# Where GpSimd's running sums stand among VectorE's operations, in a two-layer graph kernel

## The chip, the cores and the metric

The kernel runs on one core of one Trainium2 chip. A core has five engines with a queue each: TensorE (PE in the profile; its weight loads are PEld), VectorE (DVE), ScalarE (ACT), GpSimd (POOL) and SyncE (SP, which here only starts DMA transfers). Each engine works its own queue in order; between engines there are semaphores. The metric is the device time of one execution in microseconds, the median of several runs.

## The reference

For 32 batch items of 512 nodes with 512 features, two layers are computed in float32, with one adjacency matrix `adj` for all:

```python
# layer 0: attention over the graph, 8 heads of 64
q, k, v = x @ Wq + bq, x @ Wk + bk, x @ Wv + bv
scores = einsum('bihd,bjhd->bhij', q, k) / 8 + where(adj == 0, -1e9, 0)
x = layernorm(x + einsum('bhij,bjhd->bihd', softmax(scores), v))
# layer 1: graph convolution
norm_adj = adj * deg_inv_sqrt[:, None] * deg_inv_sqrt[None, :]
x = layernorm(x + norm_adj @ (x @ weight) + bias)
```

`deg` is the row sum of `adj`. The biases are part of the computation, though they are zero in the inputs.

## The kernel before

**The attention steps.** An item's eight heads are taken two at a time, four groups per item, in the order 0, 2, 1, 3. Over 32 items that makes S = 128 steps `k`, and a last round that finishes. A step treats one group in two halves (`jj`) of two key tiles each. `scores` lets TensorE multiply keys by queries into PSUM (`sc`), VectorE clips and subtracts the mask (`e<-sc,maskT`, the operation on 128x1024), and ScalarE takes the exponential in place. `values` lets TensorE multiply the exponentials of the step before by the values (`av`); when the group is done, VectorE transposes the result (`yb<-av`) and SP sends it by four DMA transfers into the item's attention output `yT`. `accumulate` lets GpSimd add the exponentials of the four key tiles up (`acc`): one addition of two tiles for the first half, two additions onto the sum for the second, all on 128x1024 in SBUF. `sums` lets TensorE turn these sums into softmax denominators, every second step. The exponentials have six buffers (`e`), the scores two (`sc`), other products three (`mm`), the attention result one (`av`).

**The pieces beside them.** Everything else is cut into pieces, Python tuples of a cost, a function and its arguments. A piece with a cost of 2.1 is one of the seven products by which `seven` makes a 512x512 matrix product out of 256x256 quarters, or one of four parts of the product with the adjacency. `values_of` and `keys_and_queries` make the next item's values, keys and queries. `turn` and `combine` transpose the item after it (`xT`) and form differences of its quarters on GpSimd. `finish(b)` gives layer 0's end for item b: `inverse` (reciprocals `inv` of the denominators), `add` (VectorE multiplies `yT` by `inv`, GpSimd adds the residual `xr`), `measure` (statistics, `st` and `mv`), `root` (`ve` and `nmu` on VectorE, `rstd` and `add` on GpSimd), `judge` (three small checks on the reciprocals), `norm` (ScalarE: `yT` normalised, then `hi`, a rounded copy scaled by the degrees), `split` (VectorE: `lo`, what `hi` left out; then GpSimd adds the bias `b1` to `yT`), `grow` (ScalarE). `convolve(b)` gives layer 1: `first` (four parts, `hi` and `lo` times `adjT`, copied by ScalarE to `zT`), `parts` (differences of `zT`'s quarters, GpSimd), `second` (seven products with the weight, added into `y` by VectorE and GpSimd), `measure`, `root` and `store`.

**What sets the order.** The order of every engine's queue is the program's. Once per item, at `at == 1`, the list `side` of pieces is written out by hand: the dictionary `beside` says after which product the pieces without cost stand. At the end of each of the four following steps, `run(side, share)` takes pieces from the list until a quarter of the remaining cost is done. It stops right after the product that reaches its due, so pieces without cost that stand behind it begin the next stretch. `accumulate` is called around `scores`: the first half's addition right before the scores of the second half, the second half's two additions right after these, in any case before the stretch.

**The end.** Item 31 has no next item. Its sums go to separate tiles, in the space of weights that are done with. Its softmax is finished in two halves, `early` for two groups and `late` for the other two (`add_half`), and its product with the adjacency goes row tile by row tile (`block`, `unload`). `held` is item 29's second layer, whose products are kept for steps 125 to 127. After the last round, lines of `run` write out the order of the rest. If the last check of a count (`bad`) is over zero, a general second kernel follows; with these inputs it does not run.

Of the kernel before, what the change touches and what calls it, by code (L numbers as in the profile page):

```python
# [9 lines left out]
F32 = mybir.dt.float32  # L10
# [3 lines left out]
AF = mybir.ActivationFunctionType  # L14
ALU = mybir.AluOpType
AX = mybir.AxisListType

P = 128
# [31 lines left out]
def unshifted(  # L50
# [29 lines left out]
    B, N, D = x.shape  # L80
    NT = N // P
    DT = D // P
    G = H // 2
    SCALE = 1.0 / HD**0.5
    tensor, vector, scalar, gpsimd = (InOrder(tc, e) for e in (nc.tensor, nc.vector, nc.scalar, nc.gpsimd))

    consts = ctx.enter_context(tc.tile_pool(name="consts", bufs=1))
    acts = ctx.enter_context(tc.tile_pool(name="acts", bufs=2))
# [14 lines left out]
    XT = consts.tile([P, 7, 2, HALF], F32, name="xT")  # L103
# [27 lines left out]
    R = {}  # L131

    def load_residual(b):

        if b < B - 2:
            t = acts.tile([P, NT, D], F32, name="xr", tag="zT", bufs=1)
            R[b] = [t[:, i, :] for i in range(NT)]
        else:
            t = XT if b == B - 2 else wk
            R[b] = [t[:, i].rearrange("p u o -> p (u o)") for i in range(NT)]  # L140
        for i in range(NT):
            nc.sync.dma_start(R[b][i], x[b, ts(i, P), :])

# [36 lines left out]
    wk = load_parts(Wk, "wk", nc.sync)  # L180
# [57 lines left out]
    bias = consts.tile([P, 2, DT], F32, name="bias")  # L238
# [111 lines left out]
            )  # L350
            scalar.activation(e, e, AF.Exp)

    def accumulate(s):


        b, g, jj = s
        n = 2 * ORDER.index(g) + jj
        a = None
        if b == B - 1:
            if n > 1:  # L360
                t, at = ((wq, 0), (wq, 2), (wq, 4), (wk, 4), (wv, 4), (XT, 4))[n - 2]
                a = t[:, at : at + 2].rearrange("p k u o -> p k (u o)")
        if a is None and (jj == 0 or b == B - 1):
            a = work.tile([P, 2, N], F32, name="acc", bufs=2)
        if a is not None:
            ACC.setdefault((b, g), []).append(a)
            gpsimd.tensor_add(a, E[s][0], E[s][1])
        else:
            for l in range(2):
                gpsimd.tensor_add(ACC[b, g][0], ACC[b, g][0], E[s][l])  # L370

    def values(s):
# [74 lines left out]
    def finish(b):  # L447


        t = {}  # L450
# [48 lines left out]
        def norm(i):  # L499
            if i == 0:  # L500
                if b < B - 1:
                    HI[b], LO[b] = (acts.tile([P, NT, D], F32R, name=k, bufs=1) for k in ("hi", "lo"))
                    LO[b] = [LO[b][:, k, :] for k in range(NT)]
                else:
                    HI[b] = acts.tile([P, NT, D], F32R, name="hi2", tag="v")
                    lo = [acts.tile([P, 2, D], F32R, name="lo2", tag="kq", bufs=5) for _ in range(2)]
                    LO[b] = [lo[k // 2][:, k % 2, :] for k in range(NT)]
            x1 = YT[b][:, i, :]
            scalar.activation(
                x1, x1, AF.Identity, bias=t["add"][:, i : i + 1], scale=t["rstd"][:, i : i + 1]  # L510
            )

            scalar.activation(HI[b][:, i, :], x1, AF.Copy, scale=dis[:, i : i + 1])

# [11 lines left out]
        def block(f):  # L526
# [3 lines left out]
            early=[(0.6, inverse, ((0,),))] + [(0, add_half, (i, 0)) for i in range(NT)],  # L530
            late=[(0.6, inverse, ((1,),))] + [(0, add_half, (i, 1)) for i in range(NT)],
            inverse=[(0.6, inverse, ((0, 1),))], add=block(add), measure=block(measure), root=[(0, root, ())],
            judge=[(0, judge, ())], norm=block(norm), split=block(split), grow=block(grow),
        )

    def weave(side, main):

        out, done = [], 0
        for k, piece in enumerate(main):
            due = len(side) * (k + 1) // len(main)  # L540
            out += side[done:due] + [piece]
            done = due
        return out + side[done:]
# [106 lines left out]
            stores=[(0, store, (n, n - n % 2)) for n in range(NT)],  # L650
        )

    def run(pieces, share=1.0):

        due = share * sum(c for c, _, _ in pieces)
        done = 0
        while pieces and (done < due or share == 1.0):
            c, f, args = pieces.pop(0)
            f(*args)
            done += c  # L660

    ORDER = (0, 2, 1, 3)
    blocks = [(b, g) for b in range(B) for g in ORDER]
# [17 lines left out]
    run(weave(masks, keys_and_queries(0, 1)))  # L681
    one, two = turns(1)
    run(one)
    side, rest, held = [], [], None
    for k in range(S + 1):
        b, at = divmod(k, G)
        if at == 1:
            run(side)
            if b:
                load_residual(b - 1)  # L690
            if b + 2 < B:
                load_x(b + 2, 0)
            if b + 1 < B:
                main, kq = values_of(b + 1) + keys_and_queries(b + 1, 0), keys_and_queries(b + 1, 1)
                turn0, turn1 = turns(b + 2) if b + 2 < B else ([], [])
                main += kq[:5]
            if b == 0:
                w1_parts = [(0, weigh_part, (w1, gpsimd, i)) for i in range(4)]
                side = main[:7] + [(0, degrees, ())] + weave(w1_parts, main[7:]) + turn0 + kq[5:] + turn1
            elif b < B - 1:  # L700
                f, c = finish(b - 1), convolve(b - 1)
                norm, split, grow = f["norm"], f["split"], f["grow"]
                add, measure = f["add"], f["measure"]

                beside = {
                    0: rest[:1], 1: rest[1:2], 2: rest[2:3], 4: rest[3:4], 5: rest[4:5] + f["inverse"],
                    6: rest[5:6] + add[:2], 7: rest[6:] + add[2:], 9: measure[:2], 10: measure[2:3],
                    11: measure[3:] + f["root"], 12: f["judge"], 13: norm[:2], 14: norm[2:3] + split[:1],
                    15: norm[3:] + split[1:2], 16: split[2:3], 17: split[3:], 18: turn0,
                }  # L710
                side = sum(([piece] + beside.get(i, []) for i, piece in enumerate(main)), [])
                side += c["first"] + c["parts"] + grow + kq[5:] + turn1[:1]
                if b < B - 2:
                    s = c["second"]
                    side += s[:1] + turn1[1:2] + s[1:4] + turn1[2:3] + s[4:5] + turn1[3:4]
                    side += s[5:6] + c["measure"][:1] + turn1[4:] + s[6:] + c["measure"][1:2]
                    rest = c["measure"][2:] + c["root"] + c["store"]
                else:
                    held = c
            else:  # L720
                f, c = finish(b - 1), convolve(b - 1)
                s, norm, split, add = held["second"], f["norm"], f["split"], f["add"]

                ending = {
                    S - 3: s[:1] + f["inverse"] + s[1:2] + add[:2] + s[2:3] + add[2:],
                    S - 2: s[3:4] + f["measure"][:2] + s[6:] + f["measure"][2:] + f["root"] + f["judge"],
                    S - 1: s[4:5] + norm[:3] + split[:1] + s[5:6] + norm[3:] + split[1:],
                    S: [],
                }


        if k == S - 2:
            load_residual(B - 1)
        if k < S:
            scores((*blocks[k], 0))
        if k:
            values((*blocks[k - 1], 0))
            values((*blocks[k - 1], 1))
            if k % 2 == 0:
                sums(blocks[k - 1][0], (k - 1) % G // 2)  # L740
        if k < S:
            accumulate((*blocks[k], 0))
            scores((*blocks[k], 1))
            accumulate((*blocks[k], 1))
        if k == 0:
            run(two)
        if k >= S - 3:
            run(ending[k])
        else:
            run(side, 1.0 / (G - (at - 1) % G))  # L750
        if k == S - 1:
            last = finish(B - 1)
            run(last["early"])

    end, e = last, convolve(B - 1)
    s, first, norm, split, block, add = c["second"], c["first"], end["norm"], end["split"], e["block"], end["late"][1:]
    run(first[:1] + end["late"][:1] + add[:2] + first[1:2] + add[2:] + first[2:3] + end["measure"][:2] + first[3:])
    run(end["measure"][2:] + end["root"] + c["parts"] + f["grow"] + held["measure"] + s[:1] + norm[:1] + s[1:2])
    run(norm[1:2] + split[:1] + s[2:3] + block[:1] + norm[2:3] + split[1:2] + s[3:4] + block[1:2] + norm[3:])
    run(split[2:3] + s[4:5] + block[2:3] + split[3:] + block[3:] + e["unload"] + e["parts"] + s[5:] + end["grow"])  # L760
    run(held["root"] + end["judge"])

# [9 lines left out]
    vector.memset(ones, 1.0)  # L774

    s, tail = e["second"], c["measure"] + c["root"] + c["store"]
    run(held["store"] + s[:1] + tail[:1] + s[1:2] + tail[1:2] + s[2:3] + tail[2:3] + s[3:4] + tail[3:5] + s[4:5])
    p = ps_mm.tile([1, 1], F32, name="mm")
    tensor.matmul(p, count, ones, start=True, stop=True)
    vector.tensor_scalar(bad, p, -1.0, float(P * B * NT * H + N), op0=ALU.mult, op1=ALU.add)  # L780
# [285 lines left out]
```

## Time and profile before

| | |
|---|---|
| Three runs | 2954.48, 2954.88, 2959.91 us (median 2954.88) |
| Profiled execution | 2955.07 us; span 2953.2 us |
| TensorE busy | 2872.4 us, 97% of the span |
| VectorE / GpSimd / ScalarE busy | 2057.9 / 1819.9 / 1062.3 us |
| One item in the middle (1074.03 to 1164.38) | 90.35 us |
| VectorE `lo`, mean of 124 | 1.464 us |
| VectorE `yT<-yT,inv`, mean of 124 | 1.249 us |
| GpSimd `acc<-acc,e`, mean of 248 | 2.534 us |
| GpSimd `acc<-e`, mean of 126 | 2.354 us |

In the profile, an operation is named by what it writes and reads (`lo<-yT,dis,hi`). All operations go through one recording helper, so they have its line, L44, and are told apart by these names. The bracket at the end of a line of the timeline gives the idle time of that engine before the line, and what ended it. A line with "x4" covers four operations with their pauses. Matmuls overlap, so their lengths add up to more than their time; the distance from start to start counts. `w` is the weight of layer 1, `b_r` its bias (`bv_r` the bias of the values). For item 31, `yT` lies in `wv`, its residual in `wk` and its `zT` and `parts` in `xT`, and the names in the trace are these.

### The profile page before, as it was taken

The numbers are of one execution on the slowest core, as the hardware profiler recorded it, in microseconds if no ns is written. First come the engines' busy times: TensorE is split into PE (matmuls) and PEld (weight loads), VectorE is DVE, ScalarE is ACT, GpSimd is POOL, SyncE is SP. The second block draws the span as 40 slices with busy tenths as digits, with TensorE's granted clock in tenths as the row PEclk, the third lists the DMA queues.
The fourth block names the chain that finished last, engine by engine and source line by source line (L and its number), as shares of the span: only waits on it lengthen the run. The fifth ranks groups of instructions, "written<-read, shape, count | busy, mean of one in ns | idle before, by whom it ended". The sixth has DMA issues, their size and how long they took to land.

```text
span 2953.2 us, 35448 instructions
## 1 busy us (share of the span) xinstructions
PE 2872.4 (97%) x12966; PEld 1878.3 (64%) x12966; DVE 2057.9 (70%) x2908; ACT 1062.3 (36%) x1342; POOL 1819.9 (62%) x1141
## 2 busy tenths in 40 slices
PE   7999999999999999999999999999999999999997
PEld 5666666666666666666666666666666666666655
DVE  7667766677667677666776676776767766677766
ACT  1233333343333333333433333333334334333243
POOL 3666566656666665666566666656665666666565
PEclk9999999999999999999999999999999999999998
DMA  5111222111222111221112221112211222211121
GB/s 130 31 26 47 49 56 50 43 36 47 54 51 47 40 47 47 57 50 43 35 49 54 50 47 40 47 47 57 48 40 39 50 54 51 46 41 47 40 47 48
DMA packets 383398, 142.40 MB, mean 48 GB/s; under 512 B 280048, under 2 KB 349680, under 8 KB 383216
## 3 DMA queue, kind: packets, MB, share of 16 engines
q1 hardware_dynamic: 381920, 138.75, 19.8%
q8 instruction: 104, 1.70, 0.2%
q10 hardware_dynamic: 1296, 1.31, 0.2%
q14 instruction: 78, 0.64, 0.1%
HBM read 72.88 MB, written 33.55 MB: 36 GB/s over the span
## 4 chain that ended last, share of the span: by engine, by line
PE 80%; DVE 15%; issue 4%; DMA 1%; ACT 0%; POOL 0%; SPq 0%; DVEq 0%; POOLq 0%; ACTq 0%
PE mm L44 50%; PE av L44 15%; PE sc L44 15%; DVE e L44 5%; DVE yT L44 3%; DVE lo L44 3%; DVE u L44 1%; DVE kq L44 1%; DMA x<-in_x_dram 0%; DVE xT L44 0%; DVE wv L44 0%; DVE st L44 0%; DVE y L44 0%; ACT yT L44 0%; ACT hi L44 0%
## 5 line engine op out<-in xcount | busy, mean ns | idle before, releaser
L44 ACT ACTIVATE e<-e 128x1024 f32<-128x1024 f32 x512 | 541.2, 1057 | 896.7 <-DVE e L44 806.4
L44 POOL TENSOR_TENSOR acc<-acc,e 128x1024 f32<-128x1024 f32 x248 | 628.5, 2534 | 126.0 <-ACT e L44 116.1
L44 DVE SCALAR_TENSOR_TENSOR e<-sc,maskT 128x1024 f32<-128x1024 f32 x512 | 601.7, 1217 | 117.3 <-PE sc L44 117.2
L44 POOL TENSOR_TENSOR acc<-e 128x1024 f32<-128x1024 f32 x126 | 296.6, 2354 | 517.3 <-ACT e L44 273.8
L44 PE MATMUL sc<-kq 64*128 64x512 f32 x2048 | 509.8, 615 | 6.4 <-DVE e L44 6.4
L44 PE MATMUL mm<-xT,wk 128*128 128x256 f32 x1792 | 474.7, 387 | 12.4 <-DVE kq L44 10.4
L44 PE MATMUL av<-e,v 128*64 128x512 f32 x2048 | 467.7, 598 | 0.0
L44 PE MATMUL mm<-xT,wq 128*128 128x256 f32 x1792 | 460.8, 380 | 0.0
L44 PE MATMUL mm<-wv,xT 128*128 128x256 f32 x1792 | 403.0, 382 | 15.2 <-DVE xT L44 11.5
L44 PEld LDWEIGHTS mm<-xT,wk 128*128 128x128 f32 x1792 | 328.0, 190 | 138.9 <-issue 74.0
L44 PEld LDWEIGHTS mm<-wv,xT 128*128 128x128 f32 x1792 | 336.3, 191 | 84.1 <-issue 26.6
L44 PEld LDWEIGHTS mm<-xT,wq 128*128 128x128 f32 x1792 | 341.1, 190 | 46.6
L44 PEld LDWEIGHTS sc<-kq 64*128 64x128 f32 x2048 | 175.9, 186 | 277.0 <-issue 187.0
L44 PEld LDWEIGHTS av<-e,v 128*64 128x64 f32 x2048 | 135.5, 136 | 315.8 <-issue 298.2
L44 POOL TENSOR_TENSOR yT<-yT,xr 128x512 f32<-128x512 f32 x120 | 161.7, 1368 | 179.2 <-DVE yT L44 173.0
L44 PE MATMUL mm<-w,zT 128*128 128x256 f32 x992 | 224.8, 379 | 0.0
L44 PE MATMUL mm<-adjT,lo 128*128 128x512 f32 x496 | 200.0, 403 | 25.2 <-DVE lo L44 25.2
L44 POOL TENSOR_TENSOR yT<-yT,b_r 128x512 f32<-128x512 f32 x124 | 170.9, 1399 | 75.4 <-DVE lo L44 75.4
L44 DVE STREAM_TRANSPOSE yb<-av 128x512 f32<-128x512 f32 x128 | 91.7, 716 | 176.7 <-PE av L44 176.7
L44 DVE SCALAR_TENSOR_TENSOR lo<-yT,dis,hi 128x512 fp32r<-128x512 f32 x124 | 181.5, 1464 | 39.8 <-ACT hi L44 39.8
L44 PEld LDWEIGHTS mm<-w,zT 128*128 128x128 f32 x992 | 188.2, 190 | 27.1 <-issue 1.5
L44 DVE TENSOR_TENSOR kq<-u,mm 128x512 f32<-128x512 f32 x128 | 86.4, 675 | 170.4 <-PE mm L44 170.3
(123 smaller groups left out, 3170.3 us busy)
## 6 DMA issues: line engine op xcount, KB each, us to landing
x<-in_x_dram SPq DMA_DIRECT2D x256, 128.0 KB, 2.9
out_dram<-y SPq DMA_DIRECT2D x128, 256.0 KB, 2.1
yT<-yb SPq DMA_DIRECT2D x496, 64.0 KB, 2.5
xr<-in_x_dram SPq DMA_DIRECT2D x120, 256.0 KB, 3.5
wv<-in_L_gnn_Wv_dram ACTq DMA_DIRECT2D x8, 128.0 KB, 4.7
wk<-in_L_gnn_Wk_dram SPq DMA_DIRECT2D x8, 128.0 KB, 4.1
wq<-in_L_gnn_Wq_dram SPq DMA_DIRECT2D x8, 128.0 KB, 4.5
yT<-in_adj_dram SPq DMA_DIRECT2D x1, 1024.0 KB, 6.6
```

Of the source, the lines that this page charges most:

```text
L44: return self.tc.keep_in_program_order(op(*args, **kwargs))
```

## The change

- **The second half's sums are put off.** For all items but the last, `accumulate` of the second half is no longer called at once. Its two additions go to a list, `pending`, one entry each, and a piece `more` issues one of them where `put_off` stands in the order. What is left is issued at the top of the next step.
- **Stretches end with all their pieces.** `run` takes whole lists. `cut` deals `side` into four lists by the number of products (pieces with a cost over 1), and the pieces behind a stretch's last product belong to that stretch.
- **The order in an item is written anew.** All of `add` comes in the first stretch, all of `norm`, `split` and `judge` in the second. The two additions put off stand: in the first stretch behind the third and the fifth product, in the second behind `measure` and `root`, in the third behind its first two products, in the fourth around the first product of `second`. `grow` goes ahead of the first layer-1 product. The statistics and stores of the item two back come together in the first stretch.
- **The end is dealt out anew.** Item 30's residual has tiles of its own (in the space of `x` and of one `kq`), and is loaded after step 123. Its `inverse` and `add` go to step 124 with the first three products of `held`; the other four, `measure`, `root`, `norm` and half of `split` to step 125; the rest of `split`, the early half of item 31, item 30's `first` and `parts` to step 126; `held`'s statistics and stores and two products of item 30's `second` to step 127. Every second `norm` of item 31 scales on VectorE instead of ScalarE.

```diff
-        else:
-            t = XT if b == B - 2 else wk
-            R[b] = [t[:, i].rearrange("p u o -> p (u o)") for i in range(NT)]
+        elif b == B - 2:
+            t = [acts.tile([P, 2, D], F32, name="xr2", tag=tag, bufs=n) for tag, n in (("x", 1), ("kq", 5))]
+            R[b] = [t[i // 2][:, i % 2, :] for i in range(NT)]
+        else:
+            R[b] = [wk[:, i].rearrange("p u o -> p (u o)") for i in range(NT)]
...
-    def accumulate(s):
+    def accumulate(s, ls=(0, 1)):
...
-            for l in range(2):
+            for l in ls:
                 gpsimd.tensor_add(ACC[b, g][0], ACC[b, g][0], E[s][l])
...
+            if b == B - 1 and i % 2:
+                vector.tensor_scalar(x1, x1, rstd, add, op0=ALU.mult, op1=ALU.add)
+            else:
+                scalar.activation(x1, x1, AF.Identity, bias=add, scale=rstd)
...
-    def run(pieces, share=1.0):
-        due = share * sum(c for c, _, _ in pieces)
-        done = 0
-        while pieces and (done < due or share == 1.0):
-            c, f, args = pieces.pop(0)
+    def run(pieces):
+        for _, f, args in pieces:
             f(*args)
-            done += c
+    def cut(pieces, counts):
+        lists = [[]]
+        left = list(counts)
+        for piece in pieces:
+            if piece[0] > 1:
+                if not left[0]:
+                    left.pop(0)
+                    lists.append([])
+                left[0] -= 1
+            lists[-1].append(piece)
+        return lists
+    pending = []
+    def more():
+        if pending:
+            accumulate(*pending.pop(0))
...
                 beside = {
-                    0: rest[:1], 1: rest[1:2], 2: rest[2:3], 4: rest[3:4], 5: rest[4:5] + f["inverse"],
-                    6: rest[5:6] + add[:2], 7: rest[6:] + add[2:], 9: measure[:2], 10: measure[2:3],
-                    11: measure[3:] + f["root"], 12: f["judge"], 13: norm[:2], 14: norm[2:3] + split[:1],
-                    15: norm[3:] + split[1:2], 16: split[2:3], 17: split[3:], 18: turn0,
+                    0: rest[:1], 1: rest[1:3], 2: put_off, 3: rest[3:4], 4: rest[4:5] + put_off,
+                    5: rest[5:6] + f["inverse"], 6: rest[6:] + add[:2], 7: add[2:],
+                    8: measure[:2] + put_off, 9: measure[2:], 10: f["root"] + put_off, 11: norm[:1],
+                    12: norm[1:2] + split[:1], 13: norm[2:3] + split[1:2], 14: norm[3:] + split[2:3],
+                    15: split[3:] + f["judge"], 16: put_off + grow[:2], 17: put_off + grow[2:], 18: turn0,
                 }
...
+                    side += put_off + s[:1] + put_off + s[1:3] + turn1[1:2] + s[3:4] + turn1[2:3] + s[4:5]
+                    side += turn1[3:4] + s[5:6] + c["measure"][:1] + turn1[4:] + s[6:] + c["measure"][1:2]
+                    shares = cut(side, (8, 8, 8, 8))
                 else:
-                    held = c
+                    held, h, last = c, s, finish(b)
+                    add = last["add"]
+                    side += h[:1] + last["inverse"] + h[1:2] + add[:2] + h[2:3] + add[2:]
+                    shares = cut(side, (8, 8, 8, 4))
...
-                ending = {
-                    S - 3: s[:1] + f["inverse"] + s[1:2] + add[:2] + s[2:3] + add[2:],
-                    S - 2: s[3:4] + f["measure"][:2] + s[6:] + f["measure"][2:] + f["root"] + f["judge"],
-                    S - 1: s[4:5] + norm[:3] + split[:1] + s[5:6] + norm[3:] + split[1:],
-                    S: [],
-                }
+                shares = [
+                    h[3:4] + f["measure"][:2] + h[6:] + f["measure"][2:] + f["root"] + h[4:5] + f["judge"] + norm[:2]
+                    + h[5:6] + split[:1] + norm[2:] + split[1:2],
+                    split[2:] + last["early"][:1] + first[:1] + add[:2] + first[1:2] + add[2:] + first[2:]
+                    + c["parts"] + f["grow"],
+                    held["measure"] + held["root"] + s[:2] + held["store"],
+                    [],
+                ]
+        while pending:
+            more()
...
-            accumulate((*blocks[k], 1))
+            if b == B - 1:
+                accumulate((*blocks[k], 1))
+            else:
+                pending += [((*blocks[k], 1), (l,)) for l in range(2)]
+        if k == S - G - 1:
+            load_residual(B - 2)
...
-        if k >= S - 3:
-            run(ending[k])
-        else:
-            run(side, 1.0 / (G - (at - 1) % G))
-        if k == S - 1:
-            last = finish(B - 1)
-            run(last["early"])
+        elif shares:
+            run(shares.pop(0))
...
-    run(first[:1] + end["late"][:1] + add[:2] + first[1:2] + add[2:] + first[2:3] + end["measure"][:2] + first[3:])
-    run(end["measure"][2:] + end["root"] + c["parts"] + f["grow"] + held["measure"] + s[:1] + norm[:1] + s[1:2])
-    run(norm[1:2] + split[:1] + s[2:3] + block[:1] + norm[2:3] + split[1:2] + s[3:4] + block[1:2] + norm[3:])
-    run(split[2:3] + s[4:5] + block[2:3] + split[3:] + block[3:] + e["unload"] + e["parts"] + s[5:] + end["grow"])
-    run(held["root"] + end["judge"])
+    run(s[2:3] + end["late"][:1] + add[:2] + s[3:4] + add[2:] + s[4:5] + end["measure"] + end["root"] + s[5:6])
+    run(norm[:2] + split[:1] + block[:1] + norm[2:3] + split[1:2] + block[1:2] + norm[3:] + split[2:3] + block[2:3])
+    run(split[3:] + block[3:] + e["unload"] + e["parts"] + s[6:] + end["grow"] + end["judge"])
...
-    run(held["store"] + s[:1] + tail[:1] + s[1:2] + tail[1:2] + s[2:3] + tail[2:3] + s[3:4] + tail[3:5] + s[4:5])
+    run(s[:1] + tail[:1] + s[1:2] + tail[1:2] + s[2:3] + tail[2:3] + s[3:4] + tail[3:5] + s[4:5])
```

More of the change, by code (lines that the diff above doesn't have):

```diff
@@ L508, in norm @@
             x1 = YT[b][:, i, :]
-            scalar.activation(
-                x1, x1, AF.Identity, bias=t["add"][:, i : i + 1], scale=t["rstd"][:, i : i + 1]
-            )
+            rstd, add = t["rstd"][:, i : i + 1], t["add"][:, i : i + 1]
+            if b == B - 1 and i % 2:
+                vector.tensor_scalar(x1, x1, rstd, add, op0=ALU.mult, op1=ALU.add)
+            else:
+                scalar.activation(x1, x1, AF.Identity, bias=add, scale=rstd)
             scalar.activation(HI[b][:, i, :], x1, AF.Copy, scale=dis[:, i : i + 1])
@@ L683, in unshifted @@
     run(one)
-    side, rest, held = [], [], None
+    shares, rest = [], []
     for k in range(S + 1):
@@ L687, in unshifted @@
         if at == 1:
-            run(side)
-            if b:
+            if 0 < b < B - 1:
                 load_residual(b - 1)
@@ L699, in unshifted @@
                 side = main[:7] + [(0, degrees, ())] + weave(w1_parts, main[7:]) + turn0 + kq[5:] + turn1
+                shares = cut(side, (6, 5, 5, 5))
             elif b < B - 1:
@@ L703, in unshifted @@
                 add, measure = f["add"], f["measure"]
+                put_off = [(0, more, ())]
                 beside = {
-                    0: rest[:1], 1: rest[1:2], 2: rest[2:3], 4: rest[3:4], 5: rest[4:5] + f["inverse"],
-                    6: rest[5:6] + add[:2], 7: rest[6:] + add[2:], 9: measure[:2], 10: measure[2:3],
-                    11: measure[3:] + f["root"], 12: f["judge"], 13: norm[:2], 14: norm[2:3] + split[:1],
-                    15: norm[3:] + split[1:2], 16: split[2:3], 17: split[3:], 18: turn0,
+                    0: rest[:1], 1: rest[1:3], 2: put_off, 3: rest[3:4], 4: rest[4:5] + put_off,
[3 more added lines that the diff above has]
+                    15: split[3:] + f["judge"], 16: put_off + grow[:2], 17: put_off + grow[2:], 18: turn0,
@@ L710, in unshifted @@
                 }
                 side = sum(([piece] + beside.get(i, []) for i, piece in enumerate(main)), [])
-                side += c["first"] + c["parts"] + grow + kq[5:] + turn1[:1]
+                side += c["first"] + c["parts"] + kq[5:] + turn1[:1]
+                s = c["second"]
                 if b < B - 2:
-                    s = c["second"]
-                    side += s[:1] + turn1[1:2] + s[1:4] + turn1[2:3] + s[4:5] + turn1[3:4]
-                    side += s[5:6] + c["measure"][:1] + turn1[4:] + s[6:] + c["measure"][1:2]
+                    side += put_off + s[:1] + put_off + s[1:3] + turn1[1:2] + s[3:4] + turn1[2:3] + s[4:5]
+                    side += turn1[3:4] + s[5:6] + c["measure"][:1] + turn1[4:] + s[6:] + c["measure"][1:2]
@@ L717, in unshifted @@
                     rest = c["measure"][2:] + c["root"] + c["store"]
+                    shares = cut(side, (8, 8, 8, 8))
                 else:
-                    held = c
-            else:
-                f, c = finish(b - 1), convolve(b - 1)
-                s, norm, split, add = held["second"], f["norm"], f["split"], f["add"]
-                ending = {
-                    S - 3: s[:1] + f["inverse"] + s[1:2] + add[:2] + s[2:3] + add[2:],
-                    S - 2: s[3:4] + f["measure"][:2] + s[6:] + f["measure"][2:] + f["root"] + f["judge"],
-                    S - 1: s[4:5] + norm[:3] + split[:1] + s[5:6] + norm[3:] + split[1:],
-                    S: [],
-                }
+                    held, h, last = c, s, finish(b)
@@ new lines, in unshifted @@
+                    add = last["add"]
+                    side += h[:1] + last["inverse"] + h[1:2] + add[:2] + h[2:3] + add[2:]
+                    shares = cut(side, (8, 8, 8, 4))
+            else:
+                f, c, last = last, convolve(b - 1), finish(b)
+                s, first, norm, split, add = c["second"], c["first"], f["norm"], f["split"], last["early"][1:]
+                shares = [
[6 more added lines that the diff above has]
+                ]
@@ L743, in unshifted @@
             scores((*blocks[k], 1))
-            accumulate((*blocks[k], 1))
+            if b == B - 1:
[4 more added lines that the diff above has]
+            load_residual(B - 2)
         if k == 0:
             run(two)
-        if k >= S - 3:
-            run(ending[k])
-        else:
-            run(side, 1.0 / (G - (at - 1) % G))
-        if k == S - 1:
-            last = finish(B - 1)
-            run(last["early"])
-    end, e = last, convolve(B - 1)
-    s, first, norm, split, block, add = c["second"], c["first"], end["norm"], end["split"], e["block"], end["late"][1:]
-    run(first[:1] + end["late"][:1] + add[:2] + first[1:2] + add[2:] + first[2:3] + end["measure"][:2] + first[3:])
-    run(end["measure"][2:] + end["root"] + c["parts"] + f["grow"] + held["measure"] + s[:1] + norm[:1] + s[1:2])
-    run(norm[1:2] + split[:1] + s[2:3] + block[:1] + norm[2:3] + split[1:2] + s[3:4] + block[1:2] + norm[3:])
-    run(split[2:3] + s[4:5] + block[2:3] + split[3:] + block[3:] + e["unload"] + e["parts"] + s[5:] + end["grow"])
-    run(held["root"] + end["judge"])
+        elif shares:
+            run(shares.pop(0))
+    end, e = last, convolve(B - 1)
+    norm, split, block, add = end["norm"], end["split"], e["block"], end["late"][1:]
+    run(s[2:3] + end["late"][:1] + add[:2] + s[3:4] + add[2:] + s[4:5] + end["measure"] + end["root"] + s[5:6])
+    run(norm[:2] + split[:1] + block[:1] + norm[2:3] + split[1:2] + block[1:2] + norm[3:] + split[2:3] + block[2:3])
+    run(split[3:] + block[3:] + e["unload"] + e["parts"] + s[6:] + end["grow"] + end["judge"])
     count = small.tile([P, 1], F32, name="count")
```

## The prediction

> **What bounds the kernel now.** I read the page's busy shares first, then the windows over one batch item, then the waits of TensorE, then the order of time around each wait. The page and one item's window (columns: length, busy us with counts, granted clock, DMA share, GB/s):
>
> ```profile
> PE 2872.4 (97%) x12966; PEld 1878.3 (64%) x12966; DVE 2057.9 (70%) x2908; ACT 1062.3 (36%) x1342; POOL 1819.9 (62%) x1141
> 1074.03:1164.38 90.35, 89.27 (x405) 58.44 (x405) 63.07 (x89) 33.19 (x42) 56.75 (x36) 1.00 0.20 47
> 1164.38:1254.74 90.36, 89.27 (x404) 58.44 (x405) 63.09 (x89) 33.20 (x42) 56.81 (x36) 1.00 0.20 47
> ```
>
> Items repeat to 0.01 us, and in each TensorE lacks work for 90.35 - 89.27 = 1.08 us. The waits view (total, times, longest) says for whom, once per item:
>
> ```profile
> PE mm L44 <- DVE lo L44: 25.2, 30, 1.1
> PE mm L44 <- DVE kq L44: 10.4, 30, 3.0
> PE sc L44 <- DVE e L44: 6.4, 4, 2.8
> ```
>
> The timeline shows why VectorE is late: first the `kq` wait, then the `lo` wait (start, length, engine):
>
> ```profile
> 1160.27 3.45 DVE L44 TENSOR_TENSOR yT<-yT,inv 128x512 f32<-128x512 f32 x2
> 1160.46 5.49 POOL L44 TENSOR_TENSOR acc<-acc,e 128x1024 f32<-128x1024 f32 x2 [1.14 <-ACT e L44]
> 1163.65 0.67 DVE L44 TENSOR_TENSOR kq<-e,mm 128x512 f32<-128x512 f32 x1
> ...
> 1092.03 5.57 POOL L44 TENSOR_TENSOR acc<-acc,e 128x1024 f32<-128x1024 f32 x2 [0.21 <-ACT e L44]
> 1093.10 2.26 DVE L44 SCALAR_TENSOR_TENSOR lo<-yT,dis,hi 128x512 fp32r<-128x512 f32 x1
> 1096.06 2.09 DVE L44 SCALAR_TENSOR_TENSOR lo<-yT,dis,hi 128x512 fp32r<-128x512 f32 x1
> 1098.21 0.50 PE L44 MATMUL mm<-adjT,lo 128*128 128x512 f32 x1 [0.82 <-DVE lo L44]
> ```
>
> Two products by `inv` take 3.45 us here and 1.29 at 1149.24, where GpSimd is idle; `lo` takes 2.26 beside a running sum and 0.75 alone (1083.16). VectorE instructions with one operand in PSUM keep 0.69 beside the same sums. The last `kq` ends 0.25 us and the last `lo` 0.82 us after TensorE needed it: that is the 1.08.
>
> [...] the lengths above are 0.65 to 0.75 plus a rest of a 2.35 us sum. When both queues are full they alternate: four `inv` products took 7.87 us at 2784.96 beside two sums and a residual addition. [...] here a 2.95 us wait is followed by matmuls of 1.91 and 1.72 us instead of 1.03 (2794.60)[...].
>
> **The change, part by part: items 1 to 29.** TensorE's order is the same there; what moves is the order on VectorE, ScalarE and GpSimd. A piece (one product of seven) takes 1.73 us of TensorE.
>
> *First stretch.* All four `inv` products now stand in it, after its seventh piece, beside residual additions only (1.27 us each). Taking turns: 4 x 0.65 + 2 x 1.27 = 5.1 us from 1149.24, so the mask step `e` starts near 1154.4 instead of 1151.43 and its halves end near 1155.6 and 1156.75. TensorE needs those score buffers at 1156.76 and 1157.7: about 1 us of slack, cost nothing. The layer norm's `rstd` now precedes the two sums on GpSimd, so these run near 1142.9 to 1147.7 (before: 1137.59 to 1142.4) and meet `u<-u,bv_r`, which has two SBUF inputs: it waits from 1143.7 to about 1145, and the matmul buffer that piece seven needs at 1146.71 is free at about 1146.9. Estimate 0.15 us an item (0 to 0.3).
>
> *Second stretch* (old time 1158.67 to 1172.5). Without the `inv` products VectorE takes `kq` at 1160.5: 0.25 us gained. The statistics (0.8 us a pair, one SBUF input) are unhindered by the first sum; `rstd` and its partner `add` end near 1167.4. The second sum follows them, 1167.4 to 1169.8, so the first `lo` (ready at 1169.0) waits 0.7 us. ScalarE's four norms with `hi` last to about 1174.2. The other three `lo` wait for at most one addition of `b1` (1.27) each: last end near 1175.1, the judging's three small instructions 0.5, `e` at 1175.7 to 1178.0. TensorE needs the two score buffers at 1178.0 and 1179.0; the halves are free at 1176.9 and 1178.0. Slack 1 us; cost nothing, bounds 0 and, if every `lo` loses a turn to one more addition, 1.3 - 1.0 = 0.3, or 2 us if several do.
>
> *Third stretch.* No `lo` is left, so first products find their operands: 0.82 us gained. GpSimd's sums stand there before `parts`, as before. *Fourth:* the order of one `xT` difference against one `y` addition; TensorE didn't wait there before; nothing. Four stores instead of three plus one are issued earlier on SP, before the `yb` transfers that follow 9 us later; nothing.
>
> Sum: 29 x (1.08 - 0.15) = 27.0 us. In item 0 the halves of the sum now stand behind other GpSimd work, up to 5.1 us, and TensorE asks for them a step later: nothing.
>
> **The end: items 30 and 31.** Let T be the end of the last attention matmul, 2883.64.
>
> *Up to T.* From 2783.3 to T are 100.34 us, of which 9.7 are lost: `kq` 2.95 plus 1.8 of slow matmuls, 1.02, 1.12, and 2.83 for `e` at 2873.77. With all `inv` products early and stretches of eight pieces the first three go, together 6.9. The last stays: the stretch of step 125 holds measures, root, norms and two `lo`, and GpSimd's `y` additions (2.5 us, behind a sum) still hold up VectorE. From the old lengths `e` starts 15.3 us after that stretch's start, and TensorE has 14.3 us of work: 2.3 us lost. In step 126 the two remaining `lo` come after both `e` and beside sums: some 3 us lost, and I add 0.7 for the clock. So 6.0 instead of 9.7. But four first products (7.45 us) and two second ones (3.46) now lie before T: T moves by 10.9 + 6.0 - 9.7 = +7.2.
>
> *After T.* Before:
>
> ```profile
> 2886.28 5.22 DVE L44 TENSOR_TENSOR wv<-wv,inv 128x128 f32<-128x128 f32 x8
> 2891.42 0.70 DVE L44 STREAM_TRANSPOSE yb<-av 128x512 f32<-128x512 f32 x1
> 2907.36 3.45 PE L44 MATMUL mm<-w,parts 128*128 128x256 f32 x8 [3.10 <-POOL parts L44]
> 2928.80 2.93 ACT L44 ACTIVATE y<-y,add,rstd 128x512 f32<-128x512 f32 x4 [3.82 <-POOL add L44]
> 2932.23 0.69 DVE L44 TENSOR_TENSOR y<-wv,mm 128x512 f32<-128x512 f32 x1 [3.35 <-ACT e L44]
> ```
>
> The transposition waited 7.8 us behind the early half's products, which go to step 126: it now starts near T+0.3. Its four transfers queue on SP behind four stores, which wait for ScalarE until about T+2.4; they land near T+6.9 (before: 2896.56, T+12.9). From landing to the layer norm's factors took 8.05 us; two `mm` evacuations and two `y` additions now stand in between, 3.0: T+18. Then 2.4 us (norm, `hi`, `lo`: 0.8 + 0.7 + 0.75 and handing over) to the first block instead of 5.8, since `parts` are long made: T+20.4 against T+26.8. Four blocks (7.4), one second product (1.7) and 1.8 for a slow clock after ten idle us: T+31.3 against 2925.20, T+41.6. The rest took 28.0; ScalarE's four stores of item 29 no longer stand before the copy of `e`, worth 3.5: T+56 against T+69.6. That is -13.5, with the move of T -6.3. Bounds: -14 if step 126 loses nothing, +4 if both `lo` wait for whole sums and the slow clock lasts.
>
> Total 27.0 + 6.3 = 33.3 from the profiled span of 2953.2: 2919.9; the median run, 2954.88, is 1.7 above that span, so 2921.6, rounded 2922. The other runs lie at 2954.48 and 2959.91.
>
> **The rivals.**
> - *Queueing eats half.* VectorE's fuller first and second stretches cost TensorE 0.5 us an item. For it: slacks are only 1 us. Against: the additions that collide are half as long as the sums. 29 x 0.58 + 4 = 21: 2934.
> - *The wait only changes place.* The second sum and `b1` additions hold `lo` so long that about 1 us an item remains; the change then does not do what it says. Only the end gains: 2949.
> - *Slower.* In the second stretch, `lo` loses turns to additions of `b1` so that `e` comes late. It decides from 2.3 us behind my schedule: 1 us of slack, 1.08 gained and 0.2 from the end. At three more additions, 3.8 us, the loss is 2.8 - 1.08 = 1.7 an item, +50 - 6: 2999. Against: pairs of waiting `lo` got through between two additions at 2882.32.
> - *The end fails:* items gain, but step 126 stalls cold: +8 there, 2936.
>
> **How the numbers follow.** Mine 0.58, half eaten 0.18, end fails 0.08, wait moved 0.07, slower 0.09. Nothing under 0.2% (6 us) can be told from no change. Mine runs from 2908 (no new wait, end -14) to 2930; taking in the half and the failed end gives 2908 to 2942. The moved wait sits at the edge of 0.2%, so: faster 0.88, same 0.03, slower 0.09.
>
> **What would show it.** Items of 89.3 to 89.6 us; TensorE's waits for `lo` and `kq` gone; `yT<-yT,inv` mean below 1.0 us, `lo` below 1.2 (before 1.25 and 1.46); sums near 2.4 instead of 2.53; the last `yb` within 1 us of the last `av`; no wait for `parts`. I'm wrong if TensorE waits for `e` or `mm` buffers once an item, or if the stretch from T exceeds 60 us.

## The result, and the profile after

The changed kernel takes 2935.02 us (median; 2934.62 to 2935.12) against 2954.68 for the kernel before: 19.7 us less, ratio 0.9929 with a 95% interval of 0.9912 to 0.9946. The forecast was 2922, with a range of 2908 to 2942. So the direction and the range held, but the gain is 60% of the forecast 33 us, about where the rival "queueing eats half" stood (2934). The prediction's own case ended at 2930; the range reached 2942 only because rivals were taken in.

The page's busy shares of the changed kernel, and the windows over two items:

```profile
PE 2871.6 (98%) x12966; PEld 1881.9 (64%) x12966; DVE 2080.2 (71%) x2910; ACT 1057.7 (36%) x1340; POOL 1812.6 (62%) x1141
1065.10:1154.94 89.84, 89.29 (x406) 58.63 (x404) 63.90 (x90) 32.96 (x42) 56.46 (x36) 1.00 0.20 48
1085.12:1175.00 89.88, 89.32 (x406) 58.67 (x406) 63.93 (x90) 33.01 (x43) 56.55 (x35) 1.00 0.20 47
```

TensorE's work is the same; an item is 0.5 us shorter, where 0.93 was forecast. The waits of TensorE show that the old two are gone and that others have come:

```profile
PE sc L44 <- DVE e L44: 17.0, 33, 2.8
PE sc L44 <- ACT hi L44: 11.2, 1, 11.2
PE mm L44 <- DVE e L44: 8.0, 32, 1.4
```

No wait for `lo` or `kq` is left. Two are new in every item: `sc` for `e` (17.0 us, 33 times), and `mm` for `e` (8.0 us, 32 times; this `e` is the one that empties a buffer of products). The 11.2 us is at the end, before the first block. The timeline shows what runs beside the late instructions. First the edge of the second and third stretch (1080.71 on), then the first stretch; lines of other operations are left out:

```profile
1080.71 1.60 DVE L44 SCALAR_TENSOR_TENSOR lo<-yT,dis,hi 128x512 fp32r<-128x512 f32 x1 [0.66 <-ACT hi L44]
1082.24 0.17 DVE L44 TENSOR_SCALAR low<-inv 128x32 f32<-128x32 f32 x1
1082.40 1.27 POOL L44 TENSOR_TENSOR yT<-yT,b_r 128x512 f32<-128x512 f32 x1 [0.63 <-DVE lo L44]
1082.44 1.27 DVE L44 SCALAR_TENSOR_TENSOR low<-inv,low 128x32 f32<-128x32 f32 x1
1083.85 2.35 DVE L44 SCALAR_TENSOR_TENSOR e<-sc,maskT 128x1024 f32<-128x1024 f32 x2
1085.12 2.26 PE L44 MATMUL sc<-kq 64*128 64x512 f32 x8 [0.37 <-DVE e L44]
...
1138.52 5.14 POOL L44 TENSOR_TENSOR acc<-acc,e 128x1024 f32<-128x1024 f32 x2
1139.65 1.78 DVE L44 TENSOR_TENSOR u<-u,bv_r 128x512 f32<-128x512 f32 x1
1142.97 1.97 PE L44 MATMUL mm<-wv,xT 128*128 128x256 f32 x8 [0.18 <-DVE e L44]
```

The check `low<-inv,low` handles 32 elements per partition and takes 1.27 us, as long as the addition of `b1` beside it, and the mask step `e`, which stands behind the checks in VectorE's queue, is late. In the first stretch `u<-u,bv_r` takes 1.78 us instead of 0.69, beside the first put-off sum. That the instruction beside them is what they wait for is tested below. The groups of operations, means in ns after the comma, say that this is so in nearly all items:

```profile
L44 DVE SCALAR_TENSOR_TENSOR lo<-yT,dis,hi 128x512 fp32r<-128x512 f32 x124 | 149.8, 1227 | 46.5 <-ACT hi L44 46.5
L44 DVE TENSOR_TENSOR u<-u,bv_r 128x512 f32<-128x512 f32 x32 | 55.5, 1736 | 1.1
L44 DVE SCALAR_TENSOR_TENSOR low<-inv,low 128x32 f32<-128x32 f32 x32 | 38.6, 1205 | 1.1
L44 POOL TENSOR_TENSOR acc<-acc,e 128x1024 f32<-128x1024 f32 x248 | 597.4, 2409 | 64.1 <-ACT e L44 54.2
```

In the kernel before, the second and the third line were:

```profile
L44 DVE TENSOR_TENSOR u<-u,bv_r 128x512 f32<-128x512 f32 x32 | 24.4, 764 | 1.1
L44 DVE SCALAR_TENSOR_TENSOR low<-inv,low 128x32 f32<-128x32 f32 x32 | 6.1, 192 | 1.1
```

**A better yardstick than idle time.** The ends of matmuls in a profile are modelled, so the idle gap before a matmul can understate a loss: TensorE's gap for `kq` was 0.25 us, but without that wait its interval is 0.55 shorter. Each step has one `av` group, and the distance from start to start of these groups shows the whole loss. In the timelines they start at 1084.81, 1107.88, 1130.31, 1152.18 and 1175.16 in the kernel before, and at 1103.79, 1126.22, 1148.51, 1170.94 and 1193.63 in the changed one. So an item divides as follows (us; the interval is named by the stretch that lies in it, and what the end of one stretch delays shows in the next interval):

| kernel | first | second | third | fourth | item |
|---|---|---|---|---|---|
| before | 21.87 | 22.98 | 23.07 | 22.43 | 90.35 |
| changed | 22.29 | 22.43 | 22.69 | 22.43 | 89.84 |
| changed, both new waits mended (below) | 21.87 | 22.43 | 21.99 | 22.42 | 88.71 |

So, measured against the last line, the old waits cost 0.55 + 1.08 = 1.63 us an item, not 1.08, and the new ones cost 0.42 + 0.70 = 1.12, not 0.15.

### The profile page after: what moved, and what is told of

It reads as the page before. It is cut to its first block, busy times and chain, and to the rows that moved or that the text cites. A ratio compares the mean times of both kernels' runs of the same rounds, so it can differ in the third digit from the quotient of the medians.

```text
span 2933.2 us, 35519 instructions
## 1 busy us (share of the span) xinstructions
PE 2871.6 (98%) x12966; PEld 1881.9 (64%) x12966; DVE 2080.2 (71%) x2910; ACT 1057.7 (36%) x1340; POOL 1812.6 (62%) x1141
## 4 chain that ended last, share of the span: by engine, by line
PE 73%; DVE 16%; ACT 6%; issue 2%; POOL 2%; DMA 1%; SPq 0%; DVEq 0%; POOLq 0%; ACTq 0%
PE mm L44 47%; PE sc L44 15%; PE av L44 12%; DVE u L44 3%; ACT yT L44 3%; DVE e L44 3%; DVE st L44 3%; ACT hi L44 2%; DVE lo L44 2%; DVE low L44 1%; POOL rstd L44 1%; ACT e L44 1%; DVE mv L44 1%; DVE kq L44 1%; DVE v L44 1%
## 5 line engine op out<-in xcount | busy, mean ns | idle before, releaser
L44 POOL TENSOR_TENSOR acc<-acc,e 128x1024 f32<-128x1024 f32 x248 | 597.4, 2409 | 64.1 <-ACT e L44 54.2
L44 PE MATMUL sc<-kq 64*128 64x512 f32 x2048 | 521.2, 623 | 17.1 <-DVE e L44 17.0
L44 POOL TENSOR_TENSOR yT<-yT,xr 128x512 f32<-128x512 f32 x124 | 193.6, 1591 | 80.6 <-DVE yT L44 80.6
L44 POOL TENSOR_TENSOR rstd<-ve,minus_half 128x4 f32<-128x4 f32 (+1 forms) x65 | 65.6, 1009 | 252.8 <-DVE nmu L44 252.7
L44 PE MATMUL mm<-adjT,hi 128*128 128x512 f32 x496 | 201.9, 407 | 0.0
```

The lines of the kernel that those rows point to most:

```text
L44: return self.tc.keep_in_program_order(op(*args, **kwargs))
```

## The experiments

Two theories. A: the new order itself is good, and two or three instructions of VectorE that it put beside GpSimd take back what it gains. B: the gain comes from putting the sums off, and what is missing is VectorE's fuller queue as such. Nine runs, each timed beside the kernel before. The executions of one variant lie up to 3.5 us apart (those of the kernel before up to 6), so a difference of 1 or 2 us says nothing.

**1. The checks elsewhere.** In the changed kernel, `judge` moves from the end of the second stretch to behind product 9 (counted from 0 over the item, the second of that stretch), where GpSimd is idle:

```diff
-                    8: measure[:2] + put_off, 9: measure[2:], 10: f["root"] + put_off, 11: norm[:1],
+                    8: measure[:2] + put_off, 9: measure[2:] + f["judge"], 10: f["root"] + put_off, 11: norm[:1],
...
-                    15: split[3:] + f["judge"], 16: put_off + grow[:2], 17: put_off + grow[2:], 18: turn0,
+                    15: split[3:], 16: put_off + grow[:2], 17: put_off + grow[2:], 18: turn0,
```

> The changed kernel, with the three checks of judge moved from the end of the second stretch to its ninth product, where GpSimd is idle between a sum and rstd. Theory A (two operations with two SBUF inputs that the new order put beside GpSimd cost most of what the items should have gained: the check low<-inv,low behind an addition of b1, and u<-u,bv_r behind a put-off sum): the check takes 0.19 us instead of 1.27, e comes 1.1 us sooner, TensorE's wait for e before the second scores goes; 0.6 us an item, 2917 (2913 to 2923). Theory B (VectorE's second stretch is simply too full; what is gained is gained by putting the sums off): the last lo is as late as before, the wait stays, 2932 to 2936.

Measured: 2912.48 us, ratio to the kernel before 0.9855 (0.9839 to 0.9872). That is 22.5 below the changed kernel, a little more than A expected and against B. The timeline, at the same place:

```profile
1073.22 1.60 DVE L44 SCALAR_TENSOR_TENSOR lo<-yT,dis,hi 128x512 fp32r<-128x512 f32 x1 [0.72 <-ACT hi L44]
1074.75 2.34 DVE L44 SCALAR_TENSOR_TENSOR e<-sc,maskT 128x1024 f32<-128x1024 f32 x2
1074.90 1.28 POOL L44 TENSOR_TENSOR yT<-yT,b_r 128x512 f32<-128x512 f32 x1 [0.63 <-DVE lo L44]
1076.66 1.99 PE L44 MATMUL sc<-kq 64*128 64x512 f32 x8
```

The last `lo` is as slow as before (1.60), but `e` follows it at once, runs beside the addition of `b1` at its full pace, and `sc` waits for nothing. The slack that the prediction counted on is there; the checks had used it up.

**2. The first stretch's sums ahead of `rstd`.** Both put-off sums go behind the first product:

```diff
-                    0: rest[:1], 1: rest[1:3], 2: put_off, 3: rest[3:4], 4: rest[4:5] + put_off,
+                    0: put_off + put_off + rest[:1], 1: rest[1:3], 3: rest[3:4], 4: rest[4:5],
```

> The changed kernel, with both put-off sums of the first stretch behind its first product, ahead of rstd on GpSimd, as before the change. Theory A: u<-u,bv_r takes 0.7 to 0.8 us instead of 1.74, TensorE's wait for the buffer of the seventh product goes; 0.4 us an item, 2923 (2920 to 2928). Theory B: sums back beside VectorE's work, no gain or a loss: 2935 to 2945.

Measured: 2922.50 us, ratio 0.9888 (0.9872 to 0.9905), 12.5 below the changed kernel. A holds:

```profile
L44 DVE TENSOR_TENSOR u<-u,bv_r 128x512 f32<-128x512 f32 x32 | 24.3, 761 | 1.1
```

**3. Nothing put off.** All sums are issued at once; stretches and order stay:

```diff
-            if b == B - 1:
-                accumulate((*blocks[k], 1))
-            else:
-                pending += [((*blocks[k], 1), (l,)) for l in range(2)]
+            accumulate((*blocks[k], 1))
```

> The changed kernel, with every second-half sum issued at once, as before the change; stretches and the new order stay. Theory A: the putting off gains nothing by itself, since the new order of add, norm and split already keeps the two-input operations away from the sums; u<-u,bv_r is free again, so faster than the changed kernel: 2925 (2920 to 2932). Theory B: the items lose what they had gained, 2945 to 2955.

Measured: 2913.94 us, ratio 0.9861 (0.9845 to 0.9877): 21.1 below the changed kernel, more than A expected. Putting the sums off, the first part of the change, costs 21 us in this order. 12.5 of them lie in the first stretch (experiment 2). Most of the other 8.6 lie at the edge of the second and third, whose interval is 22.44 instead of 22.69 here:

```profile
1065.01 1.02 POOL L44 TENSOR_TENSOR rstd<-ve,minus_half 128x4 f32<-128x4 f32 x1 [0.92 <-DVE nmu L44]
1067.94 0.75 DVE L44 SCALAR_TENSOR_TENSOR lo<-yT,dis,hi 128x512 fp32r<-128x512 f32 x1 [0.81 <-ACT hi L44]
```

Both sums of this step are over before `rstd` (they end at 1064.09); the first `lo` takes 0.75. In the changed kernel one sum follows `rstd`, and that `lo` takes 1.23:

```profile
1073.93 2.36 POOL L44 TENSOR_TENSOR acc<-acc,e 128x1024 f32<-128x1024 f32 x1
1075.61 1.23 DVE L44 SCALAR_TENSOR_TENSOR lo<-yT,dis,hi 128x512 fp32r<-128x512 f32 x1 [0.81 <-ACT hi L44]
```

**4. The new end alone.** Items 0 to 29 are those of the kernel before, with its `beside` and sums at once, and a stretch stops right after its last product (`cut_early` begins a new list there):

```diff
-                    shares = cut(side, (8, 8, 8, 8))
+                    shares = cut_early(side, (8, 8, 8, 8))
```

> The kernel before in items 0 to 29 (sums at once, old order, stretches that stop at their last product) with the new end from item 30 on. Theory A, by the prediction's sum for the end: 6 us faster than before, 2949 (2945 to 2952), items of 90.35 us. Rival: the end gives nothing and all 20 us come from the items: 2954 to 2956.

Measured: 2949.07 us, ratio 0.9979 (0.9971 to 0.9987), 6.0 below the kernel before (2955.06 in these runs). The items have the old intervals (22.99, 23.07). The end is worth about what the prediction's sum said, 6.3.

**5. The new end and the rule for stretches.** As 4, with `cut` as in the change (pieces behind a stretch's last product belong to it), the old places of the pieces and sums at once.

> The kernel before in its items (sums at once, old places of the pieces) with the new end, and with stretches that end with all their pieces: the run with the new end alone plus one rule. Theory A: the second two products by inv now stand in the first stretch, so TensorE's wait for kq goes (0.43 us an item by the distance of matmul starts), the wait for lo stays since two lo still stand beside the sums of the third stretch: 29 x 0.43 = 12 us below the new end alone, 2937 (2933 to 2941). Rival: the products by inv now delay e before the second scores, nothing gained: 2947 to 2951.

Measured: 2922.53 us, ratio 0.9888 (0.9872 to 0.9905): 26.5 below experiment 4, twice what was expected. The second interval falls to 22.43, as expected, by 0.55 rather than 0.43. The third falls too, to 22.71. In the kernel before, the second of the four `lo` stood at the head of the third stretch (1091.84); now it ends the second (1075.59 here), and the last two, though still beside the sums, come sooner:

```profile
1075.59 0.75 DVE L44 SCALAR_TENSOR_TENSOR lo<-yT,dis,hi 128x512 fp32r<-128x512 f32 x1
...
1083.16 5.15 POOL L44 TENSOR_TENSOR acc<-acc,e 128x1024 f32<-128x1024 f32 x2 [0.98 <-ACT e L44]
1084.01 2.06 DVE L44 SCALAR_TENSOR_TENSOR lo<-yT,dis,hi 128x512 fp32r<-128x512 f32 x1
1086.78 2.09 DVE L44 SCALAR_TENSOR_TENSOR lo<-yT,dis,hi 128x512 fp32r<-128x512 f32 x1
```

From the start of `av` (1075.88) to the end of the last `lo` are 12.99 us, against 13.34 before (1084.81 to 1098.15); the interval is 0.36 shorter.

Experiments 4, 5 and 3 and the changed kernel form a ladder: end -6.0, rule -26.5, new order of the pieces -8.6, putting off +21.1. This one rule brings more than the whole change.

**6. The check with one SBUF input.** Why does so small a check wait? In the changed kernel the second check reads one tensor instead of two, in the same place:

```diff
-            vector.scalar_tensor_tensor(low, inv, INV_HIGH, low, op0=ALU.is_lt, op1=ALU.mult)
+            vector.tensor_scalar(low, inv, INV_HIGH, None, op0=ALU.is_lt)
```

> The changed kernel, with the second check of judge reading one SBUF tensor instead of two, in the same place (a tensor_scalar on inv; the lower bound's check is left out). Theory A: it is the second SBUF input that waits for GpSimd: the instruction takes about 0.17 us instead of 1.27, and the time is that of the run with judge moved, 2914 (2911 to 2918). Rival: any instruction there waits, or the late lo is what counts: 2930 to 2936.

Measured: 2933.47 us, ratio 0.9927 (0.9910 to 0.9943): next to nothing. Theory A was wrong on this point. Both checks are `low<-inv` now, and the second still ends with the addition (the longest took 1.27 us, the shortest 0.17):

```profile
1080.97 1.47 DVE L44 TENSOR_SCALAR low<-inv 128x32 f32<-128x32 f32 x2
1081.13 1.27 POOL L44 TENSOR_TENSOR yT<-yT,b_r 128x512 f32<-128x512 f32 x1 [0.63 <-DVE lo L44]
```

**7. Sums in the checks' place.** Is it any instruction, then? The three checks become three sums over a constant tile:

```diff
...
-            vector.tensor_scalar(low, inv, INV_LOW, None, op0=ALU.is_gt)
-            vector.scalar_tensor_tensor(low, inv, INV_HIGH, low, op0=ALU.is_lt, op1=ALU.mult)
-            vector.tensor_reduce(FINE[:, b : b + 1], low, AX.X, ALU.add)
+            for _ in range(3):
+                vector.tensor_reduce(FINE[:, b : b + 1], sure, AX.X, ALU.add)
```

> The changed kernel, with judge's three instructions in the same place replaced by three sums over a constant tile of ones of the same size (both bound checks are left out). Theory A, corrected: what waits for GpSimd's addition of b1 there is an instruction of certain kinds, the one with two SBUF inputs and the tensor_scalar alike; a sum over one SBUF tensor does not wait. The three take 0.19 us each, e comes 1.2 us sooner, 2913 (2910 to 2918). Rival: whatever stands there waits, or the late last lo is what costs: 2930 to 2936.

Measured: 2912.52 us, ratio 0.9848 (0.9831 to 0.9864; the kernel before took 2957.39 in these runs). That is the time of experiment 1. The tile's view says that none of the 96 sums waited (shortest, median, longest in ns):

```profile
L44 DVE TENSOR_REDUCE fine<-sure x96: 171/186/188, 184.3 to 2890.8; 128x1 f32<-128x32 f32 x96
```

So it is the kind of instruction that counts, and not the place in the queue. The slow last `lo` alone costs nothing that shows: in experiment 1 too it took 1.60 us, and `sc` waited for nothing.

**8. Both mended,** the edits of 1 and 2 together.

> The changed kernel with judge moved to the ninth product and with both put-off sums of the first stretch behind its first product. Theory A: the two gains (22.5 and 12.5 us) concern different stretches and add up: 2900 (2898 to 2905), items of 88.7 us. Rival: one hides behind the other, 2908 to 2912.

Measured: 2901.42 us, ratio 0.9815 (0.9799 to 0.9832). The two gains add up to 33.6 of the 35.0. In the window over one item TensorE is busy all the time:

```profile
1069.00:1157.70 88.70, 88.70 (x407) 58.69 (x405) 62.87 (x89) 32.97 (x43) 56.24 (x36) 1.00 0.20 48
```

**9. Sums at once, checks moved,** the edits of 1 and 3 together.

> The changed kernel with all sums at once and judge moved to the ninth product: nothing is put off, only the new order and the stretches stay. Theory A: putting sums off gains nothing once judge is out of the way: as with both mended, 2901 (2898 to 2905). Rival: putting off is worth something in the second or third stretch: 3 us or more slower than the run with both mended.

Measured: 2901.57 us, ratio 0.9816 (0.9800 to 0.9833). Putting sums off is worth nothing even when nothing stands in its way. In this kernel no sum is put off, and it beats the kernel before by 53 us and the changed one by 33.

## Why the prediction was right or wrong

- **The items' bound and its causes: right, too small in size.** Both old waits went, with the products by `inv` in the first stretch and the `lo` in the second, as the prediction named it. It took their price from idle gaps, 1.08 us; by the distance of starts it is 1.63.
- **The first stretch: mis-sized.** The prediction found the collision of `u<-u,bv_r` with the put-off sum and priced it at 0.15 us. It is 0.42: the buffer came free later than reckoned, and the gap of 0.18 shows only part of it. The four `inv` products beside residual additions cost nothing, as said (they took 4.64 us).
- **The second stretch: the step that failed.** It was priced at nothing and cost 0.70 us an item. "The judging's three small instructions 0.5" is their length at the old place (0.17, 0.19 and 0.19 at 1080.73 to 1081.35 in the trace before), where GpSimd did nothing beside them but `rstd` and `add`, on four elements each. The prediction counted no wait for an addition of `b1` at the new one. The last `lo` was forecast to end near 1175.1, 16.4 us after the stretch's start; it ends 17.1 us after it (1082.3 against 1065.17), since it too ran beside an addition of `b1`. Then the checks took 1.6 us, so `e` began 18.7 us after the start instead of 17.0, past the slack of 1 us. Experiments 1 and 7 show that without this the slack suffices: worth 22.5 us.
- **The third and fourth stretch: right.** First products find their operands; the fourth interval is 22.43 in every kernel.
- **The sum.** 1.63 - 1.12 = 0.51 us an item against 0.93, over 29 items 14.8 against 27.0. Both terms were too small, and the loss by more. That the time fell into the range is in part luck: with the 1.08 of the prediction and the measured 1.12, the items would have gained nothing, and the time would have been near 2950 (estimate from these figures and the end's 6.0).
- **The end: right in the sum, less so in its parts.** Experiment 4, with the old items, gives 6.0 against 6.3. In its trace the way from the first `av` to T takes 2822.6 us against 2817.3 before, so T moved by 5.3, against 7.2 forecast. The wait at step 125 is 2.55 against 2.3. But step 126 lost some 2 us instead of 3.7: in the changed kernel's trace the group of scores after that wait took 3.14 us from start to next start instead of 1.92 (mean granted clock 0.59 from 2849 to 2853), and the four first products 8.25 instead of 7.45. The slow clock that the prediction added to its estimates shows in the traces: the mean granted clock was 0.60 after the wait of 2.95 us (2794.5 to 2798.5) and 0.54 after one of 5.11 us (2893 to 2897) in the kernel before, and 0.51 after the 11.25 us before the first block (2896.6 to 2901) in the changed one. From T to the end are 57.1 us (57.3 in the changed kernel, where T is at 2875.93) against 56; the first block starts at T+20.7 against T+20.4. The first miss helped and the second hurt, so that the sum is close is again in part luck. The chain after T shows the steps that were named, stores before the transfers of `yb` among them:

```profile
2870.32 0.61 DVE st L44
2873.96 1.02 POOL rstd L44
2875.28 2.94 ACT y L44 x4
2878.24 0.33 SPq L641
2881.54 2.44 DMA wv<-yb
2884.11 0.30 DVE wv L44 x2
```

- **The rivals.** "Queueing eats half" gave the time, 2934, but not for its reason: where the instructions that wait are moved or exchanged, a queue as full as before costs nothing (experiments 1 and 7). "Slower" had the place right, `e` late behind `lo` and additions of `b1`; `e` came 1.7 us late, short of the 2.3 from which that rival would decide.
- **The signs that it named.** The waits for `lo` and `kq` are gone, none for `parts` is left, the sums take 2.41 us, and the last `yb` starts 0.05 us after T. But an item takes 89.84 us and not 89.3 to 89.6, and the means of `yT<-yT,inv` (1.219) and `lo` (1.227) stay above their marks. The sign of being wrong came true as well: TensorE waits once an item for `e`, and once for a buffer of `mm`. By its own measure the account of the items was wrong, though the total was in range.
- **What nobody had separated.** The prediction took the change for one thing. The rule for stretches alone gives 26.5 us, and in the changed order the put-off sums take 21.1 back. The prediction priced the latter at 0.15 us an item, 4 us in all.

## What to carry to other kernels

When an instruction is moved, its old length holds only beside its old neighbours (the check took 0.19 us there and 1.27 at the new place): look up what the other engine does at the new place, for the smallest instructions too, and what is queued behind them. Price a wait by the distance between matmul starts against the same distance elsewhere, not by the gap. And try the parts of such a change apart: here one line's rule was the gain, and the part named first was a loss.

## What the runs showed of the hardware

Not only VectorE instructions with two SBUF inputs waited for a GpSimd addition in SBUF (the check took 1.27 us instead of 0.19, `lo` 1.23 instead of the 0.75 of experiment 3): in experiment 6 a `tensor_scalar` in float32 with one SBUF tensor did too (1.27 us instead of 0.17, for 32 elements). In the changed kernel's end the `tensor_scalar` of 128x512 that every second `norm` of item 31 uses took 1.51 us at 2897.92, beside an addition of `b1`, and 0.55 at 2894.99, without one. Why it waits with a single SBUF tensor is not shown.

Three kinds did not wait in these runs. The sums over one tensor in experiment 7, in the checks' place, took 0.19 us at most. Layer norm statistics took 0.70 us at most, also beside running sums (0.69 at 1157.71 in the changed kernel, beside the sum of 2.37 us at 1156.80). Of the mask steps, with one input in PSUM, none of the changed kernel's 512 took more than 1.23 us, also beside residual additions (two took 2.34 us at 1150.14).

Nor did every GpSimd instruction make VectorE wait. In the kernel before, the check with two SBUF inputs took 0.19 us at 1080.93, in the middle of GpSimd's `rstd` (128x4, 1080.23 to 1081.25), and none of the 32 took longer. Why this small instruction delays nothing is not shown.
